# A graph network on one core: the first stage's edge network moves from the first edge pass into the pass that sorts the edges

## The chip, the cores and the metric

The kernel runs on one core of a Trainium2 chip. A core has a matrix engine (TensorE, PE), three engines for elementwise work (VectorE or DVE, ScalarE or ACT, GpSimd or POOL), an engine that mostly issues transfers (SyncE, SP) and 16 DMA engines. Each engine works through its own list of instructions in order, and waits on semaphores for the others. The metric is the device time of one execution in microseconds (us), as the median of the runs.

## The reference

There are 6,250 nodes with 48 features and 200,000 edges from `src` to `dst`. Only the first layers touch the change; shortened, they are:

```python
gate = silu(edge_attr @ F1W + F1b) @ F2W + F2b            # edge_attr: 200000 x 40, gate: 200000 x 48
gate = gate + (emb[z[src]] * (emb[z[dst]] @ adapt)).sum(-1, keepdims=True)
cw   = where(d < 6, 0.5 * (cos(pi * d / 6) + 1), 0)
agg  = segment_sum(gate * h[dst] * (cw * mult[dst])[:, None], src)
h    = layernorm(h + agg / tot)
for i in range(4):                                        # attention over the edges of each src
    score = (Q[src] * K[dst]).sum(-1) + 0.1 * (edge_attr * Q[src][:, :40]).sum(-1) + log(mult)[dst]
    h = layernorm(h + leaky(concat(h, softmax_sum(score, h[dst] @ Wm)) @ Wu))
...
x = layernorm(x + h)       # then an edge MLP and two weighted sums over the edges, by dst
```

Everything is float32. The "edge network" below is the first line: 40 numbers per edge to 48 hidden numbers, Silu, and 48 gate numbers.

## The kernel before

Edges lie on 128 partitions with J = 1,564 columns each, so one column is 128 edges. The input is in order of `dst`; the sums over `src` need the edges in order of `src`. The kernel therefore sorts the edges once, and afterwards takes every sum over a node's edges as a running scan along the sorted columns.

*The counting pass* (0 to 559 us; `sort`, `counted` L309, `early` L629). DVE compares 16 columns at a time with the node numbers (L303 `ol`, L306 `oh`) and PE counts (L316). Between these steps the generator `early` is advanced one `yield` per step: it searches where the runs of equal `dst` begin (`dst_runs`), clears the table `seed` with 17 DMAs of 3.7 MB on SP's queue, orders nodes (`dst_order`), makes one row of 81 numbers per node (`node_table` L583: features times multiplicity, the projected embedding, the multiplicity; its embedding and node types are loaded on SP's queue, L589 and L601), and lets POOL scatter these rows to the place where each node's run begins in `seed` (49 indirect DMAs, line L171, from the tile `t0`).

*The scatter pass* (559 to 3,088 us; the second half of `sort`). `ranked` works on 8 columns a step: ACT copies the running counts out of PSUM (`hs`, L384), PE looks them up (`g`, L386) and adds the step's own counts (`hs_ps`, L388), DVE turns that into each edge's place (`same` L394, `pick` L397, `at` L399, `pos` L400). For every block of CS = 16 columns `whole` builds a tile `r_s` with one row per edge. `payload` loads the 40 edge numbers on SP's queue (`a_s`, L419) and ACT copies them into the rows (L421) with src, dst and distance (L422 to L424). `expanded` loads 16 columns of `seed` and spreads each run's row over the run: ACT copies into PSUM (`run_v`, L286), DVE scans (`xf`, L269), and ACT copies the result into the rows (L676). A row has 124 floats (496 B): src, dst, distance, 40 edge numbers, 81 spread numbers. POOL then scatters the 16 columns one by one to their places in the DRAM table `rows_s` (L171). `whole` is called one block ahead of its scatters, and `r_s` has three buffers. Beside it runs `beside`: the rows of the dst order (`a_d`, `r_d`, `rows_d`), clears of the `spread` tables, and 49 scatters of node embeddings in the middle. The order on each engine is fixed at build time by a scheduler, except where `tc.keep_in_program_order` is written; each engine's queue, SP's DMA issues included, is worked through in that order.

*The first edge stage* (3,088 to 4,281 us; `gated_sums`, tile pool `e0`) reads the sorted rows in parts of C = 40 columns. PE turns the 40 edge numbers and the embedding product of two columns at a time (L954), ACT copies them out (L956), PE applies the first layer to 8 columns (L963), ACT does Silu (L965), DVE copies the two embedding products under it (L966), PE applies the second layer (L973), and DVE multiplies the gate numbers in PSUM with the edge's features (L975). Before that, DVE and ACT make the cutoff factor `u` (L915 to L923), POOL multiplies it into the features (L924), and DVE scans the sources' embeddings (`qf`, L269), multiplies and sums them (L931, L933). After it DVE scans the sums (`sf`, L986), and ACT copies them to `st` (L989), written to DRAM from ACT's queue. ACT also copies the 40 edge numbers and the product to `ra` (L909), which is written to the table `rows_a` of 41 floats a row (L934). The next part's opening (`begun`) is advanced one step per `turn`.

*Attention* (4 layers, to 13.9 ms) reads `rows_a` in parts of 40 columns on SP's queue, with one POOL gather of 128 rows per column from `tab_kv` (L166), and uses the 40 edge numbers on PE (L1125). The edge MLP and the two weighted sums follow. They are not touched.

## Time and profile before

| | |
|---|---|
| median of 3 runs | 21,866.9 us (21,861.03 to 21,871.99) |
| the profiled execution: its own time, its span | 21,773.17 us, 21,771.4 us |
| busy share of the span: PE, DVE, ACT, POOL | 27%, 37%, 22%, 64% |
| mean granted TensorE clock | 0.62 of full speed |
| counting pass, 0 to 559.4 us: busy DVE, ACT, POOL | 383.3, 26.8, 141.8 us |
| scatter pass, 559.4 to 3,088 us: busy PE, DVE, ACT, POOL | 836.7, 1,413.2, 820.2, 1,574.9 us |
| first edge stage, 3,088 to 4,281 us: busy PE, DVE, ACT, POOL | 811.2, 891.9, 584.7, 136.6 us |
| attention and its node stages, 4,281 to 13,840 us: busy POOL, DVE | 6,955.8, 3,784.3 us |
| rest, 13,840 to 21,771 us: busy POOL, DVE | 5,045.5, 1,618.3 us |

The stages follow each other in time, and each has its own limit, so a busy share of the whole span says little. In the profile L12 means line 12 of the kernel; a row such as "L421 ACT r_s" is the group of instructions that this line issued on that engine. "PEld" is the loading of weights into TensorE. "issue" as the reason of a wait means that the profile shows nothing that the engine waited for, "remote" or "an unknown queue" that the releaser is not in the record.

### The profile page before, as it was taken

The page shows a single profiled execution, that of the slowest core. Times are in us where ns is not written, and L with a number is a line of the kernel's source. Part 1 is how long each engine was busy: PE and PEld are TensorE (multiplying, and loading weights), DVE is VectorE, ACT ScalarE, POOL GpSimd, SP SyncE. Part 2 cuts the span into 40 slices and gives each one's busy share as a digit, 9 for nine tenths or more (in the row PEclk, how much of TensorE's full clock was granted, in tenths as well). Part 3 has the DMA queues.
Part 4 walks back from the last instruction along what each step waited for, and adds up shares of the span by engine and source line. Part 5 has one row for each costly group of instructions (what it writes and reads, how often), then busy time and mean ns, then how long its engine had stood idle before and what let it go on. Part 6 is the DMA issues. An engine that isn't in the chain of part 4 may idle for free.

```text
span 21771.4 us, 87599 instructions
## 1 busy us (share of the span) xinstructions
PE 5782.7 (27%) x19726; PEld 3494.4 (16%) x19726; DVE 8090.9 (37%) x16421; ACT 4790.3 (22%) x6563; POOL 13854.5 (64%) x13410
## 2 busy tenths in 40 slices
PE   2332346622223222322223222245545200000000
PEld 2332334410002000200002000133333100000000
DVE  6554557644333344334333334322222211111001
ACT  0332334411111111111111111133333200001111
POOL 2666641177775777577775777644444577777777
PEclk9999995555555555555555555566666655555555
DMA  5455544332222222222222222211111111111111
GB/s 157 165 172 134 172 169 180 151 87 88 86 83 66 86 87 88 60 89 88 86 81 70 86 85 88 57 40 43 43 46 44 33 36 34 36 36 36 36 36 36
DMA packets 873560, 1792.36 MB, mean 82 GB/s; under 512 B 365490, under 2 KB 546658, under 8 KB 868034
## 3 DMA queue, kind: packets, MB, share of 16 engines
q1 hardware_dynamic: 349038, 860.63, 12.0%
q0 software_dynamic: 427520, 547.67, 10.8%
q10 hardware_dynamic: 96468, 378.32, 4.6%
q8 instruction: 167, 2.74, 0.1%
q14 instruction: 367, 3.01, 0.0%
HBM read 1144.48 MB, written 641.17 MB: 82 GB/s over the span
## 4 chain that ended last, share of the span: by engine, by line
POOL 43%; issue 21%; DVE 10%; another core or an unknown queue 10%; PE 9%; ACT 6%; DMA 1%; ACTq 0%; SPq 0%; POOLq 0%; DVEq 0%
POOL t L166 41%; PE ps L1207 2%; PE ps L1214 2%; PE ps L1222 1%; ACT run_v L286 1%; POOL own L166 1%; DVE qf L269 1%; DVE ol L303 1%; PE g L386 1%; DVE sf L986 1%; PE ps_t L1200 1%; ACT st L1230 1%; ACT st L989 1%; DVE run_v L267 1%
## 5 line engine op out<-in xcount | busy, mean ns | idle before, releaser
L166 POOL DMA_INDIRECT t<-tab_kv,other x6256 | 6576.9, 1051 | 2112.8 <-issue 2069.6
L166 POOL DMA_INDIRECT t<-tab_x,other x4692 | 4788.3, 1021 | 2605.8 <-issue 1457.2
L1124 PE MATMUL ka<-t,ident 128*128 128x480 f32 (+2 forms) x1264 | 1213.3, 1063 | 6798.6 <-DMA t<-tab_kv,other 6015.1
L1126 DVE TENSOR_TENSOR q<-qf,ka 128x480 f32<-128x480 f32 (+2 forms) x632 | 677.9, 1074 | 4126.9 <-issue 3358.9
L171 POOL DMA_INDIRECT rows_s<-r_s,scratch x1564 | 1527.9, 977 | 967.8 <-ACT r_s L421 466.7
L1124 PEld LDWEIGHTS ka<-t,ident 128*128 128x128 f32 x1264 | 316.3, 310 | 7520.9 <-issue 4273.1
L269 DVE TENSOR_TENSOR_SCAN qf<-fac,run_v 128x480 f32<-128x480 f32 (+1 forms) x943 | 1028.8, 1092 | 654.0 <-DVE run_v L267 409.8
L841 PE MATMUL cy_ps<-ident,last_s 128*48 128x128 f32 (+1 forms) x4 | 1.6, 406 | 4523.5 <-DVE last_s L275 4523.5
L1156 ACT COPY st<-m 128x40 f32<-128x40 f32 (+3 forms) x164 | 42.8, 261 | 5233.9 <-DVE sc L1129 4099.3
L386 PE MATMUL g<-hs,olt 128*128 128x49 f32 x3128 | 759.0, 418 | 1231.1 <-ACT hs L384 860.3
L286 ACT COPY run_v<-q 128x480 f32<-128x480 f32 (+1 forms) x943 | 851.7, 916 | 503.1 <-DVE qf L269 197.8
L1125 PE MATMUL ka<-r,tenth 128*128 128x400 f32 (+2 forms) x1264 | 959.7, 863 | 0.0
L1216 DVE TENSOR_SCALAR h<-ps,b 128x512 f32<-128x512 f32 x391 | 293.6, 751 | 1725.5 <-PE ps L1207 829.7
L386 PEld LDWEIGHTS g<-hs,olt 128*128 128x128 f32 x3128 | 696.1, 327 | 1283.6 <-ACT hs L384 893.0
L1304 DVE TENSOR_TENSOR run_v<-t,w_ps 128x480 f32<-128x480 f32 (+3 forms) x164 | 142.1, 912 | 1832.6 <-DMA t<-tab_x,other 1832.6
L267 DVE SCALAR_TENSOR_TENSOR run_v<-last_s,ns,run_v 128x12 f32<-128x12 f32 x480 | 98.0, 219 | 1934.1 <-issue 1280.6
L924 POOL TENSOR_TENSOR r<-r,u 128x1920 f32<-128x1920 f32 (+3 forms) x41 | 135.5, 3305 | 1034.3 <-DVE u L923 931.1
L269 DVE TENSOR_TENSOR_SCAN sf<-dec,run_v 128x480 f32<-128x480 f32 (+5 forms) x820 | 728.1, 921 | 36.1 <-remote 14.9
L841 PEld LDWEIGHTS cy_ps<-ident,last_s 128*48 128x48 f32 (+1 forms) x4 | 0.5, 126 | 4524.3 <-ACT st L1310 2261.5
L1207 PE MATMUL ps<-at,w 112*128 112x512 f32 x782 | 539.5, 779 | 506.8 <-ACT h L1209 428.3
L1155 ACT COPY st<-sf 128x1960 f32<-128x1960 f32 (+3 forms) x164 | 620.8, 3785 | 13.3 <-DVE run_v L267 11.0
L1148 DVE TENSOR_TENSOR run_v<-t,es 128x480 f32<-128x480 f32 (+2 forms) x656 | 616.1, 961 | 9.9 <-issue 5.1
(395 smaller groups left out, 15085.7 us busy)
## 6 DMA issues: line engine op xcount, KB each, us to landing
q<-spread_s SPq DMA_DIRECT2D x190, 960.0 KB
state_a<-st ACTq DMA_DIRECT2D x152, 1000.0 KB
r<-rows_a SPq DMA_DIRECT2D x152, 820.0 KB
state_h<-st ACTq DMA_DIRECT2D x114, 960.0 KB
t<-tab_kv,other POOLq DMA_INDIRECT x6256
r<-rows_s SPq DMA_DIRECT2D x38, 2480.0 KB
t<-tab_x,other POOLq DMA_INDIRECT x4692
seed<-zeros SPq DMA_DIRECT2D x17, 3726.0 KB
```

Of the source, the lines that this page charges most:

```text
L166: return nc.gpsimd.indirect_dma_start(out=dst, out_offset=None, in_=table, in_offset=bass.IndirectOffsetOnAxis(ap=idx, axis=0))
L171: i = nc.gpsimd.indirect_dma_start(out=table, out_offset=bass.IndirectOffsetOnAxis(ap=idx, axis=0), in_=src, in_offset=None)
L269: V.tensor_tensor_scan(flat[:, f0 * wid:(f0 + n) * wid], fac[:, :n * wid], v.rearrange("p f c -> p (f c)")[:, :n * wid], 0.0, OP.mult, OP.add)
L286: return lambda v, f0, n: S.copy(v, by_feature(src[:, :, f0:f0 + n]))
L386: T.matmul(g[:, b0 + b, :], olt[:, b0 + b, :], hs[:, b, :], start=True, stop=True)
L1124: T.matmul(ka, ident, t[:, j0:j1, 0:H], start=True, stop=False)
L1125: T.matmul(ka[:, :, 0:RBF], tenth, r[:, j0:j1, 0:RBF], start=False, stop=True)
L1126: V.tensor_mul(q[:, j0:j1, :], by_column(qf)[:, j0:j1, :], ka)
L1148: V.tensor_mul(v, by_feature(t[:, :, H + 1 + f0:H + 1 + f0 + n]), es[:, None, :].to_broadcast([P, n, wid]))
L1155: S.copy(st[:, :, 0:H + 1], by_column(sf))
L1207: T.matmul(ps, w1, at, start=True, stop=True)
L1214: T.matmul(ps, w2, h1, start=True, stop=True)
```

## The change

- The edge network moves from `gated_sums` into `expanded`. A copy of the edge numbers, transposed on the host (80 rows: two neighbouring columns of 40 numbers, by column pair, by partition), is a new input. Each block of 16 columns loads its part of it on SP's queue (`at_e`, 80 partitions), and PE, ACT, PE, ACT make the 48 gate numbers and copy them into the row tile. The first layer loses the extra rows that carried the embedding product through, and the second layer keeps one row for its bias.
- A row of `rows_s` grows from 124 to 172 floats (496 to 688 B): 40 edge numbers, then src, dst and distance, 48 gate numbers, 81 spread numbers. `a_s` and `a_d` go from two buffers to one, `r_d` from three to two.
- `gated_sums` works on parts of 32 columns (50 parts), loads floats 40 to 171 of each row (528 of 688 B), and has no PE work. POOL multiplies the cutoff factor into the features as before, and in a second instruction adds the embedding product to the gate numbers. DVE multiplies the two from SBUF. The opening of the next part (`gates`) is issued as a whole before the sums of the present one.
- `rows_a` has 40 floats a row. It is now written in the first attention layer, which loads its 160 B of each row from `rows_s` and writes them on from ACT's queue.
- In the counting pass `node_table` runs directly behind `dst_order`; its loads of the embedding and the node types go through ACT's queue, and `t0` lies in another pool. The number of `yield`s between the steps changes (22 and 18 before, 6 and 20 after).

```diff
     W0 = H + G + 1
-    WS, WD = 3 + RBF + W0, 3 + EF
-    rows_a = dram.tile([EP, RA], F32, name="rows_a")
+    WS, WD = RBF + 3 + H + W0, 3 + EF
+    O = {"s": RBF, "d": 0}
+    rows_a = dram.tile([EP, RBF], F32, name="rows_a")
     seed = dram.tile([EP + NP, W0], F32, name="seed")
...
-        a = by_columns(pool, wid, attr.shape[1], f"a_{k}", CS)
+        a = by_columns(pool, wid, attr.shape[1], f"a_{k}", CS, bufs=1)
         tc.keep_in_program_order(nc.sync.dma_start(a, pj(attr)[:, s, :]))
-        r = by_columns(pool, wid, rows[k].shape[1], f"r_{k}", CS, bufs=3)
-        tc.keep_in_program_order(S.copy(r[:, :, 3:3 + attr.shape[1]], a))
-        S.copy(r[:, :, 0], ends[k][:, s])
-        S.copy(r[:, :, 1], ends["d" if k == "s" else "s"][:, s])
-        S.copy(r[:, :, 2], ew[:, s])
+        r = by_columns(pool, wid, rows[k].shape[1], f"r_{k}", CS, bufs=3 if k == "s" else 2)
+        o, f0 = (RBF, 0) if k == "s" else (0, 3)
+        tc.keep_in_program_order(S.copy(r[:, :, f0:f0 + attr.shape[1]], a))
+        S.copy(r[:, :, o], ends[k][:, s])
+        S.copy(r[:, :, o + 1], ends["d" if k == "s" else "s"][:, s])
+        S.copy(r[:, :, o + 2], ew[:, s])
...
-    def node_table(pool, psum):
+    def node_table(pool, psum, t0):
         V.tensor_mul(t0[:, :, 0:H], x, mult[:, :, None].to_broadcast([P, NB, H]))
         S.copy(t0[:, :, W0 - 1], mult)
         both = pool.tile([NEL, 2, G], F32, name="both")
-        nc.sync.dma_start(both[:, 0], A["L0_gnn_emb"])
+        nc.scalar.dma_start(both[:, 0], A["L0_gnn_emb"])
...
-            nc.sync.dma_start(z, bass.AP(tensor=types.tensor, offset=types.offset + b0 * P, ap=[[0, P], [1, 7 * P]]))
+            nc.scalar.dma_start(z, bass.AP(tensor=types.tensor, offset=types.offset + b0 * P, ap=[[0, P], [1, 7 * P]]))
...
-        for _ in range(22):
+        t0 = hp.tile([P, NB, W0], F32, name="t0")
+        yield from node_table(hp, psum, t0)
+        for _ in range(6):
             yield
         next(search)
-        yield from node_table(hp, psum)
-        for _ in range(18):
+        for _ in range(20):
...
-    def expanded(pool, psum):
+    def expanded(pool, psum, net_psum):
+        hid = [pool.tile([2 * H + 1, 4, P], F32, name=f"hid{i}", bufs=1) for i in range(2)]
+        for t in hid:
+            V.memset(t, 1.0)
         fac = factors(pool, "fac", SG, CS)
         first = pool.tile([P, 1, W0], F32, name="first", bufs=1)
         gather(first[:, 0, :], tab0[:], ends["d"][:, 0:1])
@@ -668,7 +671,18 @@
             wid = r.shape[1]
             t = by_columns(pool, wid, W0, "seeds", CS)
             tc.keep_in_program_order(nc.sync.dma_start(t, pj(seed[0:EP, :])[:, j0:j0 + wid, :]))
-            fac_, x0 = fac(j0 // CS, nsd[:, j0:j0 + wid]), 3 + RBF
+            at = pool.tile([2 * RBF, CS // 2, P], F32, name="at_e")[:, :wid // 2, :]
+            tc.keep_in_program_order(nc.sync.dma_start(at, A["edge_attr_40_t"][:, j0 // 2:(j0 + wid) // 2, :]))
+            for i, (k0, n) in enumerate(blocks(4, 0, wid // 2)):
+                ps = net_psum.tile([2 * H, 4, P], F32, name="ps_1")[:, :n]
+                T.matmul(ps, f1w, at[:, k0:k0 + n], start=True, stop=True)
+                hi = hid[i % 2][:, :n]
+                S.activation(hi[0:2 * H], ps, AF.Silu, bias=f1b)
+                ps = net_psum.tile([P, 4, 2, H], F32, name="ps_2")[:, :n]
+                for k in range(n):
+                    T.matmul(ps[:, k], hi[:, k, :], f2, start=True, stop=True)
+                S.copy(r[:, 2 * k0:2 * (k0 + n), RBF + 3:RBF + 3 + H], ps.rearrange("p k t w -> p (k t) w"))
+            fac_, x0 = fac(j0 // CS, nsd[:, j0:j0 + wid]), RBF + 3 + H
...
+    C0 = 32
     def gated_sums(ep, psum):
-        hid = [ep.tile([2 * H + 3, 4, P], F32, name=f"hid{i}", bufs=1) for i in range(2)]
-        for t in hid:
-            V.memset(t, 1.0)
         prev, f = segments_begin("s", ep)
-        factor = factors(ep, "fac")
+        factor = factors(ep, "fac", cols=C0)
         before = {"q": first_rows(ep, tab_q, "first"), "s": None, "prev": prev}
-        X0 = 3 + RBF
...
+        N0, X0 = 3, 3 + H
+        B0 = X0 + H
+        parts = [(c0, C0) for c0 in range(0, J - C0, C0)] + [(J - J % C0, J % C0 - 12), (J - 12, 12)]
+        def gates(c):
+            c0, wid = parts[c]
             s = slice(c0, c0 + wid)
-            r = by_columns(ep, wid, WS, "r")
-            nc.sync.dma_start(r, pj(rows["s"][:])[:, s, :])
-            q = by_columns(ep, wid, H, "q")
+            r = by_columns(ep, wid, WS - RBF, "r", C0, bufs=3)
+            nc.sync.dma_start(r, pj(rows["s"][:])[:, s, RBF:])
+            q = by_columns(ep, wid, H, "q", C0)
             nc.sync.dma_start(q, pj(spread["s"][0:EP, :])[:, s, :])
             before["prev"] = segments_chunk(c0, wid, r, before["prev"])
-            ra = by_columns(ep, wid, RA, "ra")
-            S.copy(ra[:, :, 0:RBF], r[:, :, 3:X0])
             fac, first = factor(c, ns[:, s]), ns[:, c0:c0 + 1]
-            kept[c] = r, ra, fac, first
-            yield
-            u = ep.tile([P, C], F32, name="u")[:, :wid]
+            u = ep.tile([P, C0], F32, name="u")[:, :wid]
             V.tensor_scalar(u, r[:, :, 2], 1.0 / (2.0 * CUT), None, op0=OP.mult)
-            n = ep.tile([P, C], F32, name="n", bufs=1)[:, :wid]
+            n = ep.tile([P, C0], F32, name="n", bufs=1)[:, :wid]
             V.tensor_scalar(n, u, ROUND, None, op0=OP.add)
             V.tensor_scalar(n, n, -ROUND, None, op0=OP.add)
             V.tensor_sub(u, u, n)
             V.tensor_mul(u, u, u)
             V.tensor_scalar(u, u, -1.0, 1.0, op0=OP.mult, op1=OP.add)
             V.scalar_tensor_tensor(u, r[:, :, 2], CUT, u, op0=OP.is_lt, op1=OP.mult)
-            nc.gpsimd.tensor_tensor(r[:, :, X0:X0 + H], r[:, :, X0:X0 + H], u[:, :, None].to_broadcast([P, wid, H]),
...
+            x_ = r[:, :, X0:B0]
+            nc.gpsimd.tensor_tensor(x_, x_, u[:, :, None].to_broadcast([P, wid, H]), op=OP.mult)
+            qf = by_features(ep, G, wid, "qf", C0, bufs=1)
+            runs(psum, qf, fac, first, before["q"], G, copied(q), cols=C0)
             before["q"] = kept_last(ep, qf, "last_q")
-            yield
...
+            V.tensor_mul(q[:, :, :G], by_column(qf), r[:, :, B0:B0 + G])
+            pair = ep.tile([P, C0], F32, name="pair")[:, :wid]
+            V.tensor_reduce(pair, q[:, :, :G], AX.X, OP.add)
+            g = r[:, :, N0:X0]
+            nc.gpsimd.tensor_tensor(g, g, pair[:, :, None].to_broadcast([P, wid, H]), op=OP.add)
+            return r, fac, first
+        def sums(c, r, fac, first):
+            c0, wid = parts[c]
+            v = by_features(ep, H + 1, wid, "v", C0)
+            S.copy(v[:, H, :], r[:, :, WS - RBF - 1])
+            V.tensor_mul(by_column(v)[:, :, 0:H], r[:, :, N0:X0], r[:, :, X0:B0])
             if before["s"] is not None:
                 V.scalar_tensor_tensor(v[:, :, 0], before["s"], first, v[:, :, 0], op0=OP.mult, op1=OP.add)
-            sf = by_features(ep, H + 1, wid, "sf", bufs=1)
+            sf = by_features(ep, H + 1, wid, "sf", C0, bufs=1)
             flat, values = (t.rearrange("p f c -> p (f c)") for t in (sf, v))
             for f0 in range(0, H + 1, FG):
                 j = slice(f0 * wid, min(f0 + FG, H + 1) * wid)
                 V.tensor_tensor_scan(flat[:, j], fac[:, :j.stop - j.start], values[:, j], 0.0, OP.mult, OP.add)
             before["s"] = kept_last(ep, sf, "last_s")
-            st = by_columns(ep, wid, H + 1, "st", bufs=1)
+            st = by_columns(ep, wid, H + 1, "st", C0)
             S.copy(st, by_column(sf))
-            nc.scalar.dma_start(pj(state0[0:EP, :])[:, s, :], st)
+            nc.scalar.dma_start(pj(state0[0:EP, :])[:, c0:c0 + wid, :], st)
+        ahead = gates(0)
+        for c in range(len(parts)):
+            now = ahead
+            if c + 1 < len(parts):
+                ahead = gates(c + 1)
+            sums(c, *now)
         return f, before["prev"], before["s"]
...
-                r = by_columns(ep, wid, RA, "r")
-                nc.sync.dma_start(r, pj(rows_a[:])[:, s, :])
+                r = by_columns(ep, wid, RBF, "r")
+                if l == 0:
+                    nc.sync.dma_start(r, pj(rows["s"][:])[:, s, 0:RBF])
+                    nc.scalar.dma_start(pj(rows_a[:])[:, s, :], r)
+                else:
+                    nc.sync.dma_start(r, pj(rows_a[:])[:, s, :])
...
-                    T.matmul(ka[:, :, 0:RBF], tenth, r[:, j0:j1, 0:RBF], start=False, stop=True)
+                    T.matmul(ka[:, :, 0:RBF], tenth, r[:, j0:j1, :], start=False, stop=True)
...
+        elif name == "edge_attr_40_t":
+            a = _np.ascontiguousarray(padded(a, EP, 0).reshape(P, J // 2, 2 * RBF).transpose(2, 1, 0))
```

## The prediction

> **What bounds the kernel now.** I read the page first: its chain of waits and its costliest groups.
>
> ```profile
> PE 5782.7 (27%) x19726; PEld 3494.4 (16%) x19726; DVE 8090.9 (37%) x16421; ACT 4790.3 (22%) x6563; POOL 13854.5 (64%) x13410
> ...
> POOL t L166 41%; PE ps L1207 2%; PE ps L1214 2%; PE ps L1222 1%; ACT run_v L286 1%; POOL own L166 1%; DVE qf L269 1%; DVE ol L303 1%; PE g L386 1%; DVE sf L986 1%; PE ps_t L1200 1%; ACT st L1230 1%; ACT st L989 1%; DVE run_v L267 1%
> ...
> L171 POOL DMA_INDIRECT rows_s<-r_s,scratch x1564 | 1527.9, 977 | 967.8 <-ACT r_s L421 466.7
> ```
>
> POOL is busy for 64% of the span, but almost all of that is gathers in the attention and edge stages after 4,281 us, which keep their form. The third line is the scatter pass (559 to 3,088 us), the stage into which the edge network moves: 1,564 scatters of 0.977 us, and before 88 of its 98 blocks POOL waits for ACT's last write of the block's row tile (L421), 466.7 us in total. Then the table of stretches (columns: stretch, length, busy us and count for PE, PEld, DVE, ACT, POOL, then TensorE clock, DMA share, GB/s):
>
> ```profile
> 559.00:1000.00 441.00, 149.22 (x822) 138.04 (x822) 250.96 (x854) 145.43 (x328) 271.73 (x278) 1.00 0.50 167
> 1000.00:1500.00 500.00, 175.46 (x968) 162.12 (x967) 296.52 (x1010) 170.28 (x381) 315.09 (x323) 1.00 0.53 173
> ...
> 1900.00:3088.00 1188.00, 405.50 (x2232) 375.09 (x2232) 683.25 (x2332) 398.48 (x896) 746.28 (x764) 1.00 0.50 163
> ...
> 3200.00:4200.00 1000.00, 691.84 (x2343) 474.14 (x2342) 751.70 (x1215) 500.05 (x608) 115.64 (x34) 0.59 0.45 181
> ```
>
> The first three rows are the scatter pass: no engine is full, PE is busy 35% of the time and its clock is 1.00. The last is the first edge stage (`gated_sums`, 3,092 to 4,281 us): DVE is busy 75% of the time, PE 69%, at clock 0.59. Its chain of waits repeats at L989 at 3,618.44, 3,648.33 and 3,678.20 us: 29.9 us for each part of 40 columns. Third, the timeline of one block of the scatter pass:
>
> ```profile
> 1006.04 0.32 PE L388 MATMUL hs_ps<-oh,ol 128*128 128x49 bf16 x4 [1.27 <-DVE oh L306]
> ...
> 1011.79 0.95 POOL L171 DMA_INDIRECT rows_s<-r_s,scratch  x1 [0.30 <-issue]
> 1015.13 0.32 ACT L384 COPY hs<-hs_ps 128x196 f32<-128x196 f32 x1 [9.76 <-remote]
> ...
> 1015.66 0.92 ACT L676 COPY r_s<-xf 128x432 f32<-128x432 f32 x1
> ...
> 1016.48 0.74 ACT L421 COPY r_s<-a_s 128x640 f32<-128x640 f32 x1
> ...
> 1017.50 0.96 POOL L171 DMA_INDIRECT rows_s<-r_s,scratch  x1 [4.75 <-ACT r_s L421]
> ```
>
> PE issues its four short `hs_ps` products at 1006.04. ACT can read them only at 1015.13, after 9.76 us of waiting, 2.4 us after the last scatter of the burst has ended (1012.74). From there it takes two copies to finish the next row tile, and the next burst starts at 1017.50. The chain shows the same wait ending at 1040.34 and 1065.12. I cannot see why PE's signal is late; I only see that it is tied to the end of the burst. So a block costs the burst (16 scatters 1.26 us apart, 20.2 us), 2.4 us until ACT is released, and what ACT still has to write: 24.8 us. ACT's idle 9.76 us are the slack in which added work can hide; work ordered behind that wait is paid in full. Last, the groups of the edge stage between 3,200 and 4,200 us:
>
> ```profile
> L973 PE MATMUL ps<-f,hid 99*128 99x96 f32 x1337 | 327.5, 426 | 114.3 <-DVE hid L966 114.3
> ...
> L963 PE MATMUL ps<-at,f1w 82*98 82x512 f32 x336 | 289.5, 960 | 1.5 <-ACT at L956 1.5
> ...
> L924 POOL TENSOR_TENSOR r<-r,u 128x1920 f32<-128x1920 f32 x34 | 117.5, 3457 | 895.1 <-DVE u L923 842.3 <-ACT run_v L286 52.8
> L966 DVE COPY hid<-ps 2x512 f32<-2x512 f32 x168 | 117.1, 697 | 175.3 <-ACT hid L965 172.1
> L965 ACT ACTIVATE hid<-ps,f1b 96x512 f32<-96x512 f32 x169 | 115.1, 681 | 31.4 <-PE ps L963 23.2 <-ACT v L945 7.9
> ...
> L931 DVE TENSOR_TENSOR q<-qf,r 128x1280 f32<-128x1280 f32 x33 | 86.6, 2624 | 0.0
> ...
> L933 DVE TENSOR_REDUCE ra<-q 128x40 f32<-128x1280 f32 x33 | 49.1, 1487 | 1.0
> L275 DVE COPY last_q<-qf 128x32 f32<-128x32 f32 x34 | 39.9, 1173 | 0.0
> ...
> L275 DVE COPY last_s<-sf 128x49 f32<-128x49 f32 x34 | 7.1, 208 | 1.2
> ```
>
> **The change part by part.** *Edge stage, the saving.* Twenty transposes, five copies, five hidden layers, five Silu, the `hid` copies (L966), twenty f2 products, five PSUM products (L975), the 1.56 us `ra` copy and the `rows_a` write all go. The part is now 32 columns and DVE is its longest engine. Per part: other and ns 0.54 (0.171+0.152+0.221); seven u operations 1.29; qf scans of 384, 384 and 256 elements, interpolated between 1.135 (480) and 0.821 (320), 2.59; three first-column updates at 0.23, 0.69; last_q 0.2; q product 0.8×2.624=2.10; reduction 0.8×1.487=1.19; the new v product from SBUF, 1,536 elements at L931's 2.05 ns, 3.15; its first column 0.32; sf scans 4×0.95+0.24=4.04; last_s 0.21. Sum 16.3 us. POOL's product grows from one to two, each 0.8×3.457=2.77 us. The trace shows what POOL can do to DVE: `last_q` takes 1.173 us against 0.208 for the larger `last_s`, because it starts while L924 runs and ends with it (3607.54). In the new order the v product and scans of the previous part stand right behind the reduction that starts POOL's second product, so I charge one full POOL product: 19.1 us. Before: 1,564/40×29.9=1,169 us. After: 1,564/32×19.1=933. Saving 236 us. Bounds: no collision, 16.3 us, saves 372; DVE only as full as now (75%), 21.7 us, saves 109.
>
> Here a rule speaks against the change. The Trainium skill (SBUF — State Buffer, "Who interferes with whom") says that a DVE instruction with two SBUF inputs contends with a GpSimd instruction that reads SBUF, and the later one fully blocks. The new v product and the sf scans are of that kind. By it both POOL products would be charged, 21.8 us a part, and the saving would be about 100 us. The trace has only the copy meeting POOL.
>
> The row load reads 132 of 172 floats, 4,096 pieces of 528 B. Row and data of the part come to 3.75 MB in 19.1 us, 196 GB/s, against 181 now; it is loaded ahead, so I charge 0. If pieces are slow, the load caps the saving (rival 3).
>
> *Scatter pass, the cost.* Per block of 16 columns: one SP load (80 partitions × 4 KB, 327 KB), two f1w products, two Silu, eight f2 products, two copies of 384 elements from PSUM. Estimated from the rows: f1w two records, 1.71 us in the chain at clock 0.59, so 1.0 at 1.00; Silu 0.68; f2 1.84 for eight records, so 1.1; copy 0.80 (run_v's 432 take 0.89). A group in series is 3.6 us, a block 7.2. The Silu and the copies wait for PE, and behind them in ACT's queue stand the `hs` and xf copies, for which PE's next products and the next burst wait; f1w waits for `at_e` with `g` and `hs_ps` behind it. Lower bound: all of it inside ACT's 9.76 idle us, 0. Upper: all in series behind the release, 98×7.2=706 us. A gain is excluded: nothing that delays PE's signal is removed. In between I use the written order of ACT, which repeats every five blocks. Behind the release, beyond today's copies, stand: one xf copy (0.93); nothing; a PSUM copy that first waits for f2 and an xf copy (3); a whole run of copies, xf, Silu and next-row numbers (about 11); nothing. Mean 3 us. I add 0.3 for the wider rows: 688 B instead of 496, while a scatter now lands 2.1 us after issue (bounds 0 and 0.8, if landing scales by 1.39). So 3.3 us × 98 = +323 us. POOL issues each scatter as before.
>
> On SP, `at_e` waits for PE and the row input `a_s` (now one buffer) for ACT's copy; behind them stand the krow and lrow loads that DVE's comparisons need. Those already wait for DVE two steps earlier, so 0; if SP stalls, the load time of 2 to 3 us a block shows, inside the same upper bound. The extra issue, 98×0.32=31 us, lies on an idle queue.
>
> *Counting pass.* `node_table` comes earlier, and its emb and types loads leave SP (where they stood behind 17 clears of 3.7 MB until 213 us) for ACT's queue. DVE sets the end of this pass: after 420 us it is busy 130.9 of 139. Its work is unchanged, so 0; bounds −40 (the two 18 to 20 us waits for PE beside the seed scatters) and +25 (types landing late beside the clears in front of DVE's comparisons). Four missing small weight loads: 0 to −3, taken as 0.
>
> *Attention, first layer.* 41 loads of 5,120 pieces of 160 B replace contiguous ones, and the `rows_a` write of the edge stage comes here, on ACT's queue, with all ACT work of a part behind it. A part takes 55.6 us (18 in 1,000 us), POOL is busy 76%, ACT 17%, DMA share 0.29. Taken +5; bounds 0 and 41×2.5=100 if the pieces delay gathers.
>
> Sum: −236+323+0+5=+92 us, 21,773+92=21,865 for an execution like the profiled one. That one lies 94 us below the median of 21,867 (three runs within 11 us); on the median's scale 21,959.
>
> **The rivals.**
> 1. *The network hides (faster).* ACT's 9.76 us are longer than 7.2. If the network runs entirely in front of the late `hs`, a block pays 0 to 1 us. Then −236+50+5: 21,690; with the uncollided edge stage 21,550. For it: DVE, the fullest engine there (59%), gets nothing new. Against: the order of ACT above. The turn is at 236/98=2.4 us a block.
> 2. *Much slower, by the TensorE clock.* At 69% PE load the clock fell from 1.00 to 0.59 within 100 us of the edge stage; at 35% it held. The network takes PE to about 52% of a block. At 0.59 PE would need (8.7+4.2)/0.59=21.9 of 25 us; three more us a block, 98×3=294, on top: 22,250. Or handshakes slip behind the late signal one after another, up to the bound of 706: 22,340. Against: 35% held for 2,500 us.
> 3. *The edge stage gains nothing much*, since loads or the POOL collision set 22 us a part: saving 100, with the scatter cost 323: 22,095.
>
> **How the numbers follow.** Scatter cost and edge saving decide. Forecast (2.5 to 5 us a block) 0.42; rival 1 0.34; rival 2 0.14; rival 3 0.10. About 0.2% (44 us) is what a measurement here tells from no change. With 236 us saved the forecast runs from +14 to +259, so I put a fifth of it, 0.08, within 44 us, and 0.34 above. Slower: 0.34+0.14+0.10=0.58; faster 0.34; same 0.08. Range: 21,590 (rival 1, a little above its best) to 22,350 (rival 2's bound); the forecast alone 21,850 to 22,250.
>
> **What would show it.** Right: bursts of `rows_s` 27 to 30 us apart instead of 24.8, POOL's wait behind L421 replaced by ACT writes of r_s from PSUM or xf, and its total rising from 467 to about 790 us; the edge stage's `st` 18 to 20 us apart with the v product stretched beside POOL. Wrong: bursts still 25 us apart (rival 1), a granted clock below 0.9 before 3,000 us (rival 2), or `st` 22 us and more apart with idle DVE waiting for r (rival 3). The whole would be wrong if PE's signal were no longer tied to the burst's end: then the pass could approach its 20.2 us bursts, and no row of this trace prices that.

## The result, and the profile after

The changed kernel takes 21,917.8 us (median of 13 runs, 21,903.2 to 21,930.3), the kernel before 21,867.3 us (13 runs, 21,856.0 to 21,896.1) beside it: ratio 1.0020, 95% interval 1.0012 to 1.0029. It is 50 us slower, where the prediction said 92. The profiled execution of the changed kernel took 21,915.7 us, close to its median; that of the kernel before lay 94 us below its own, so I took a second profile of the kernel before (run r1: 21,868.1 us, span 21,866.3) and compare with that one.

From the page of the changed kernel: busy time, the clock in 40 slices, and the group of the scatters.

```profile
PE 5653.7 (26%) x18944; PEld 3361.3 (15%) x18944; DVE 8082.2 (37%) x16312; ACT 4678.3 (21%) x6585; POOL 14029.4 (64%) x13469
...
PEclk9999999965555555555555555567666655555555
...
L170 POOL DMA_INDIRECT rows_s<-r_s,scratch x1564 | 1533.2, 980 | 1349.7 <-ACT hs L383 703.3
```

The clock stays at 1.00 until the attention begins (slice 9); with the edge network gone from it, the edge stage runs without PE. POOL's wait in front of the scatters is now put down to ACT's `hs` copy at L383, 703.3 us, where L421 stood with 466.7. The stretches (columns as before: PE, PEld, DVE, ACT, POOL, clock, DMA share, GB/s):

```profile
1000.00:1500.00 500.00, 267.97 (x1167) 211.44 (x1164) 253.84 (x867) 177.36 (x399) 268.90 (x274) 1.00 0.53 170
...
1900.00:3475.00 1575.00, 811.35 (x3520) 638.97 (x3519) 757.57 (x2586) 539.51 (x1201) 851.36 (x869) 1.00 0.53 162
...
3700.00:4375.00 675.00, 0.92 (x2) 0.36 (x2) 672.81 (x1034) 215.74 (x263) 218.95 (x76) 1.00 0.68 198
```

In the scatter pass PE is busy 54% (35% before), DVE 51% (58% in the second profile of before). In the edge stage (last row) DVE is busy all the time.

First and last scatter, for the second profile of the kernel before and for the changed kernel (count, shortest, median, longest ns, first and last start):

```profile
L171 POOL DMA_INDIRECT rows_s<-r_s,scratch x1564: 952/958/1457, 556.4 to 3135.1; - x196
```

```profile
L170 POOL DMA_INDIRECT rows_s<-r_s,scratch x1564: 954/960/1491, 562.6 to 3475.4; - x196
```

| stage, us | before (r1) | after | difference | predicted |
|---|---|---|---|---|
| counting pass, to the first scatter | 556.4 | 562.6 | +6 | 0 |
| scatter pass, first to last scatter | 2,578.7 | 2,912.8 | +334 | +323 |
| edge stage, to its last `st` copy | 1,194.6 | 900.1 | −295 | −236 |
| rest of the span | 17,536.6 | 17,538.4 | +2 | +5 |

So the parts have the signs that were predicted, the scatter pass has its size too, and what the prediction lacked is 59 us in the edge stage; the two passes took 17 of them back.

One block of the scatter pass in the changed kernel, from the timeline:

```profile
1013.03 1.99 PE L683 MATMUL ps<-f,hid 97*128 97x96 f32 x8
...
1014.81 1.92 PE L678 MATMUL ps<-at_e,f1w 80*96 80x512 f32 x2
...
1020.40 0.96 POOL L170 DMA_INDIRECT rows_s<-r_s,scratch  x1 [0.30 <-issue]
1023.55 0.49 ACT L684 COPY r_s<-ps 128x384 f32<-128x384 f32 x1 [9.94 <-remote]
...
1024.66 2.02 PE L683 MATMUL ps<-f,hid 97*128 97x96 f32 x8 [7.94 <-ACT hid L680]
...
1026.72 0.49 ACT L684 COPY r_s<-ps 128x384 f32<-128x384 f32 x1 [2.11 <-PE ps L683]
1027.10 0.32 ACT L383 COPY hs<-hs_ps 128x196 f32<-128x196 f32 x1
...
1027.62 0.94 ACT L690 COPY r_s<-xf 128x432 f32<-128x432 f32 x1
...
1028.44 0.73 ACT L421 COPY r_s<-a_s 128x640 f32<-128x640 f32 x1
...
1029.45 0.95 POOL L170 DMA_INDIRECT rows_s<-r_s,scratch  x1 [8.09 <-ACT r_s L421]
```

PE issues the first group's f2 products (L683) and the second group's f1w products (L678) by 1014.81, some 2 us long each. ACT's copy of the first gate numbers (L684) starts only at 1023.55, 2.2 us after the last scatter of the burst has ended. From there ACT needs the copy, a Silu, a second round through PE (L683, 2.02 us), another copy, `hs`, an xf copy and the attribute copy: 5.9 us from the release to the next burst, where it was 2.4 before (5.9 to 8.9 us over the blocks between 1,000 and 1,500 us that begin with such a wait). The median block is 29.2 us (25.0 in r1).

The edge stage between 3,600 and 4,300 us (line, operation, forms, count, busy us, mean ns, idle before):

```profile
L958 DVE TENSOR_TENSOR_SCAN sf<-fac,v 128x384 f32<-128x384 f32 x155 | 279.6, 1825 | 0.0
L944 POOL TENSOR_TENSOR r<-r,pair 128x1536 f32<-128x1536 f32 x39 | 121.0, 3102 | 173.4 <-DVE pair L942 173.4
...
L951 DVE TENSOR_TENSOR v<-r 128x1536 f32<-128x1536 f32 x39 | 108.6, 2785 | 0.0
L936 POOL TENSOR_TENSOR r<-r,u 128x1536 f32<-128x1536 f32 x38 | 107.5, 2828 | 293.4 <-DVE u L934 293.4
L940 DVE TENSOR_TENSOR q<-qf,r 128x1024 f32<-128x1024 f32 x39 | 73.3, 1880 | 0.0
...
L928 DVE TENSOR_SCALAR n<-u 128x32 f32<-128x32 f32 x39 | 54.0, 1384 | 0.0
...
L929 DVE TENSOR_SCALAR n<-n 128x32 f32<-128x32 f32 x39 | 6.6, 170 | 0.0
```

A scan of 384 elements takes 1.825 us on average, where I expected 0.95, and L928, a 32-element operation, 1.384 us, while its twin L929 takes 0.170. Both are means of two kinds: 56 of the 155 scans take 3.4 us on average, the others about 0.95, and 19 of the 39 L928 take 2.66 us, the others 0.17. The parts differ too, 21.5 and 14.6 us in turn, 18.25 on average. Two stretches in time order show why, first one with a held L928, then one with held scans:

```profile
3660.05 2.80 POOL L944 TENSOR_TENSOR r<-r,pair 128x1536 f32<-128x1536 f32 x1 [4.13 <-DVE pair L942]
...
3660.23 2.65 DVE L928 TENSOR_SCALAR n<-u 128x32 f32<-128x32 f32 x1
...
4001.02 4.47 DVE L958 TENSOR_TENSOR_SCAN sf<-fac,v 128x384 f32<-128x384 f32 x3
...
4001.18 3.38 POOL L944 TENSOR_TENSOR r<-r,pair 128x1536 f32<-128x1536 f32 x1 [4.75 <-DVE pair L942]
...
4014.77 3.48 POOL L936 TENSOR_TENSOR r<-r,u 128x1536 f32<-128x1536 f32 x1 [10.21 <-DVE u L934]
...
4015.56 2.73 DVE L274 COPY last_q<-qf 128x32 f32<-128x32 f32 x1
4018.21 1.88 DVE L940 TENSOR_TENSOR q<-qf,r 128x1024 f32<-128x1024 f32 x1
```

In the first, L928 starts at 3660.23 beside a POOL product and ends at 3662.88, just behind it (3662.85). In the second, POOL's product of 1,536 elements runs from 4001.18 to 4004.56; the three scans that DVE has at the same time take 4.47 us instead of 2.8. The second POOL product ends at 4018.25, and the 32-element copy `last_q`, started at 4015.56, ends at 4018.29 with it. Counted one by one between 3,600 and 4,300 us, 77 POOL products hold up 77 DVE instructions: 56 long scans, 19 times L928, once a short scan and once `last_q`. The `qf` scans of 384 elements, which read one input from PSUM, are not held: 0.95 us in the 9 of the whole stage that meet a POOL product, 0.94 in the 85 that don't.

The runs below come from several sessions, and in some of them every kernel, the one before included, took about 18.7 ms instead of 21.8 ms; so each run is held only against the kernel before of its own session, and stage against stage of such sessions. I call the 21.8 ms sessions *late* and the 18.7 ms sessions *prompt*, for a reason that the runs show. The expectations call them "the first chip" and "the second chip", which turned out wrong: one chip was prompt in one session (r5 to r8) and late in another (r15, r16).

### The profile page after: what moved, and what is told of

Its sections match the earlier page's. It is cut to its first block, busy times and chain, and to the rows that moved or that the text cites. A ratio compares the mean times of both kernels' runs of the same rounds, so it can differ in the third digit from the quotient of the medians.

```text
span 21913.9 us, 86031 instructions
## 1 busy us (share of the span) xinstructions
PE 5653.7 (26%) x18944; PEld 3361.3 (15%) x18944; DVE 8082.2 (37%) x16312; ACT 4678.3 (21%) x6585; POOL 14029.4 (64%) x13469
## 3 DMA queue, kind: packets, MB, share of 16 engines
q0 software_dynamic: 452544, 586.11, 11.4%
## 5 line engine op out<-in xcount | busy, mean ns | idle before, releaser
L170 POOL DMA_INDIRECT rows_s<-r_s,scratch x1564 | 1533.2, 980 | 1349.7 <-ACT hs L383 703.3
L268 DVE TENSOR_TENSOR_SCAN qf<-fac,run_v 128x480 f32<-128x480 f32 (+6 forms) x970 | 1030.4, 1065 | 642.8 <-DVE run_v L266 374.3
L285 ACT COPY run_v<-q 128x480 f32<-128x480 f32 (+6 forms) x970 | 855.8, 895 | 560.3 <-DVE qf L268 254.9
L683 PE MATMUL ps<-f,hid 97*128 97x96 f32 x1564 | 399.2, 434 | 858.9 <-ACT hid L680 806.7
```

What stands on the lines that cost most here:

```text
L170: i = nc.gpsimd.indirect_dma_start(out=table, out_offset=bass.IndirectOffsetOnAxis(ap=idx, axis=0), in_=src, in_offset=None)
L268: V.tensor_tensor_scan(flat[:, f0 * wid:(f0 + n) * wid], fac[:, :n * wid], v.rearrange("p f c -> p (f c)")[:, :n * wid], 0.0, OP.mult, OP.add)
L285: return lambda v, f0, n: S.copy(v, by_feature(src[:, :, f0:f0 + n]))
L683: T.matmul(ps[:, k], hi[:, k, :], f2, start=True, stop=True)
```

## The experiments

**r1: the kernel before once more**, without an edit.

> The kernel before once more, unchanged, for a second profile. The profiled execution of the prediction lay 94 us below the median of its kernel. If that execution was an odd one, this profile has a span near 21,865 us and shows in which stages the 94 us lie; if profiles of this kernel always read 0.4% short, the span is again near 21,775 us. Its ratio to the kernel before is 1.000.

21,871.0 us, ratio 1.000 (0.999 to 1.0009); the span is 21,866.3. The profile on which the prediction rests was a short execution: of the 95 us between the two, 51 lie in the scatter pass (2,527.7 and 2,578.7 us), 3 in the edge stage, 44 in small pieces behind it, and the counting pass is 3 shorter. Putting the 94 us on top of the sum as a constant was right for the kernel's time.

**r2, r3: blocks of 8 columns**, in the kernel before and in the changed one.

```diff
-CS = 16
+CS = 8
```

> Kernel before with blocks of 8 columns instead of 16 in the scatter pass (195 bursts of 10.1 us instead of 98 of 20.2 us). Theory 1, PE's signal is held only once a burst has lasted some 12 us: no hs copy waits longer than about 2 us in a burst, the pass takes 195 x (10.1 + 1 to 2) = 2,160 to 2,360 us instead of 2,529, the kernel 170 to 370 us less. Rival, the signal is held until the end of any burst: 195 x (10.1 + 4.6) = 2,870 us, the kernel about 340 us more.

> Changed kernel with blocks of 8 columns. Theory 1 (held only in bursts over 12 us): the handovers of the edge network meet no held signal, the pass takes 195 x (10.1 + 1 to 3) = 2,160 to 2,550 us instead of 2,913, the kernel 21,370 to 21,750. Rival (held until the end of any burst): 195 x (10.1 + 5 to 9) = 2,940 to 3,700 us, the kernel 21,950 or more.

r2: 22,195.4 us, ratio 1.0149 (1.0132 to 1.0166). r3: 21,830.5 us, ratio 0.9982 (0.9972 to 0.9991).

```profile
L171 POOL DMA_INDIRECT rows_s<-r_s,scratch x1564: 952/958/1255, 561.3 to 3469.9; - x196
```

```profile
L170 POOL DMA_INDIRECT rows_s<-r_s,scratch x1564: 954/961/1440, 557.2 to 3390.0; - x196
```

For the kernel before, the rival is right: the pass takes 2,909 us, 330 more. Short bursts don't set PE's signals free. But the two kernels differ: the changed one, with more work, is 76 us shorter in the same pass (2,833), and 80 us shorter than with blocks of 16. Neither of my two theories says that. What POOL waits for between 1,000 and 1,500 us, in r2 and then in r3 (us, times, longest):

```profile
POOL rows_s L171 <- ACT hs L384: 159.1, 17, 9.4
```

```profile
POOL rows_s L170 <- ACT hs L383: 111.4, 21, 7.9
...
POOL rows_s L170 <- ACT r_s L684: 32.1, 7, 4.6
```

Two bursts of the kernel before follow each other at once and then POOL waits 9.4 us, while the changed one waits about 5 us in front of most bursts. So the two written orders give different numbers of pauses; that this is what makes the passes differ is argued, not shown.

**r4: the edge network without PE.** ACT's two Silu and two copies a block stay, on constant tiles; the gate numbers are constants.

```diff
-                T.matmul(ps, f1w, at[:, k0:k0 + n], start=True, stop=True)
+                ps = const1[:, :n]
...
-                for k in range(n):
-                    T.matmul(ps[:, k], hi[:, k, :], f2, start=True, stop=True)
+                ps = const2[:, :n]
```

> Changed kernel; the edge network's products on PE are left out of the scatter pass, ACT's two Silu and two copies a block stay and read constant tiles in PSUM (the gate numbers are constants). The load of the transposed edge numbers stays. Theory: the network costs by its handovers with PE that fall behind the late signal, so a block falls from 29.2 to 25 to 26 us and the pass by 310 to 410 us, the kernel to about 21,550. Rival: ACT's added time or the wider rows cost it, a block stays at 28 to 29 us and the kernel within 100 us of 21,918.

21,810.7 us, ratio 0.9976 (0.9966 to 0.9985).

```profile
L170 POOL DMA_INDIRECT rows_s<-r_s,scratch x1564: 954/960/1661, 557.8 to 3396.1; - x196
```

The pass takes 2,838 us, 75 less than with PE's products. By whole kernels, each against the kernel before of its own session, it is 114 us less (64 faster than before instead of 50 slower; the profiled execution of r4 lies 19 us above its median). So my theory, that the cost is PE's answers falling behind the late signal, covers 75 to 114 of 334 us. The median block is 25.9 us, as the theory said, but the blocks are no longer alike: four in a row take 20.2, 45.1, 26.8 and 20.6 us. I read this so: where a row tile is finished before the burst ends, the next burst follows at once, no pause lets PE's signals through, and the next but one waits the longer. The trace supports it only in part. Of the time that ACT spends in the scatter pass in waits over 2 us that end without a releaser, 784 of 1,226 us end in a pause of POOL (over 1 us) in r1, 872 of 975 in the changed kernel and 710 of 1,203 in r4. The others end while a burst runs, as this one in r1:

```profile
1200.83 0.96 POOL L171 DMA_INDIRECT rows_s<-r_s,scratch  x1 [0.31 <-issue]
...
1201.75 0.32 ACT L384 COPY hs<-hs_ps 128x196 f32<-128x196 f32 x1 [11.36 <-remote]
...
1202.09 0.96 POOL L171 DMA_INDIRECT rows_s<-r_s,scratch  x1 [0.30 <-issue]
```

**r5 to r8, r9 to r12, r13 to r16.** I meant these to split the rest, but the sessions of r5 to r14 were prompt, and only that of r15 and r16 was late, like that of r1 to r4. They are told by kernel.

*The changed kernel itself in a prompt session (r9).*

> The changed kernel once more, unchanged. On the first chip (before: 21,870 us) PE's signals come late while POOL scatters, on the second (before: 18,731 us) they did not. If this run falls on the second chip: the scatter pass pays only what doesn't fit beside POOL's bursts, 2,220 us as in the kernel without the pair product against 2,096 (+124), the edge stage saves 294, the kernel is about 170 us faster than before (18,560). On the first chip: 21,918 again, scatter pass 2,913, edge stage 900.

18,574.3 us against 18,720.2: ratio 0.9921 (0.9905 to 0.9938). Here the change makes the kernel 146 us faster. For the stages of before in a prompt session I use r6, which was as fast as the kernel before (first r6, then r9):

```profile
L171 POOL DMA_INDIRECT rows_s<-r_s,scratch x1564: 953/959/1647, 421.6 to 2517.9; - x196
```

```profile
L170 POOL DMA_INDIRECT rows_s<-r_s,scratch x1564: 954/960/1702, 444.6 to 2648.2; - x196
```

The scatter pass is 2,096.3 us before and 2,203.6 after, +107 instead of +334; the edge stage is 899.3 us, the same as in late sessions (1,193.5 in r6); the counting pass ends at 444.6 instead of 421.6, +23. Together −164, and the whole −146: the profiled execution of r6 lies 23 us above the median of the kernel before in r9's session. In the counting pass DVE waits 29 us for the gathers of the search in r9, 4.8 us in r6. I put that to the fewer `yield`s between the steps; no run changes them alone:

```profile
DVE got L566 <- DMA got<-steps,at: 19.0, 1, 19.0
DVE got L566 <- DMA got<-dst_steps,at: 10.3, 1, 10.3
```

*One buffer (r6).* The kernel before with `a_s` and `a_d` single and `r_d` double.

```diff
-        a = by_columns(pool, wid, attr.shape[1], f"a_{k}", CS)
+        a = by_columns(pool, wid, attr.shape[1], f"a_{k}", CS, bufs=1)
...
-        r = by_columns(pool, wid, rows[k].shape[1], f"r_{k}", CS, bufs=3)
+        r = by_columns(pool, wid, rows[k].shape[1], f"r_{k}", CS, bufs=3 if k == "s" else 2)
```

> Kernel before, with the one buffer of the changed kernel for the edge numbers (a_s, a_d) and two for r_d; nothing else. If the single buffer costs the time (SP waits for ACT's copy with the krow and lrow loads behind it), the pass grows by 100 us or more, to 2,680 us and more, and the kernel to 21,970 or more. If it doesn't, the kernel stays within 30 us of 21,867.

18,735.4 us, ratio 1.0002 (0.9992 to 1.0012), prompt. The buffers cost nothing there; in a late session it was not tried.

*No edge network at all (r5, r10, r13, r15).* The rows stay 688 B wide, DVE fills the 48 gate numbers with a constant; nothing of the network is computed.

```diff
-            at = pool.tile([2 * RBF, CS // 2, P], F32, name="at_e")[:, :wid // 2, :]
...
-                S.copy(r[:, 2 * k0:2 * (k0 + n), RBF + 3:RBF + 3 + H], ps.rearrange("p k t w -> p (k t) w"))
+            V.memset(r[:, :, RBF + 3:RBF + 3 + H], 0.5)
```

> Changed kernel with the whole edge network left out of the scatter pass (no load of the transposed numbers, no PE, no Silu, no copies; the 48 gate numbers are filled with a constant by DVE). Rows stay 688 B wide, the attribute tile stays single. Theory, ACT's four added operations a block (2.4 us of work on the in-order queue that also carries the hs copies) are the cost: a block falls back to 25 to 25.5 us, the pass to about 2,600 us, the kernel to 21,580 to 21,620. Rival, the wider rows or the single buffer cost it: the pass stays above 2,750 us and the kernel above 21,740.

> Changed kernel without the edge network in the scatter pass, the 48 gate numbers a constant. On the second chip its pass was as long as that of the kernel before (2,094 against 2,096 us): the wider rows were free there. On the first chip, if the network (and not the rows) makes the pass longer: 2,580 to 2,650 us against 2,913, the kernel at 21,580 to 21,650. If the wider rows do: above 2,800 and 21,800. On the second chip again: 18,462.

> Changed kernel without the edge network in the scatter pass, meant for the first chip (before: 21,870 us). If the network makes the pass longer there: 2,580 to 2,650 us against 2,913, the kernel at 21,580 to 21,650. If the wider rows do: above 2,800 and 21,800. On a chip like the second: 18,455 and a pass of 2,090.

> As the run of this kernel before it. On the first chip: 2,580 to 2,650 us of scatter pass and a kernel of 21,580 to 21,650 if the network makes the pass longer there, above 2,800 and 21,800 if the wider rows do. On another chip: about 18,460 and 2,090, and the point stays open.

Prompt: 18,461.9 us (ratio 0.9856, 0.9840 to 0.9873), 18,454.8 (0.9859, 0.9842 to 0.9875) and 18,475.8 (0.9857, 0.9842 to 0.9873), with passes of 2,094, 2,086 and 2,094 us. The wide rows cost nothing there; all 107 us of the prompt pass are the network. Late (r15): 21,688.7 us against 21,757.6, ratio 0.9969 (0.9953 to 0.9984). First r10, then r15:

```profile
L170 POOL DMA_INDIRECT rows_s<-r_s,scratch x1564: 956/960/1573, 441.0 to 2527.1; - x196
```

```profile
L170 POOL DMA_INDIRECT rows_s<-r_s,scratch x1564: 954/960/1642, 556.3 to 3306.5; - x196
```

In the late session the pass without the network still takes 2,750 us, between my two expectations: 163 less than the changed kernel and 171 more than the kernel before, both as profiled in other sessions. Its blocks repeat as 35.4, 25.0, 30.8, 26.4 and 20.7 us. Held against its own session the split is another. By whole kernels the network is worth 119 us (50 slower than before with it, 69 faster without), hardly more than PE's products alone in r4 (114). And the kernel before was 116 us faster in that session than in that of r1, while the span behind the edge stage was only 54 to 63 us shorter (17,473 us in r15 and 17,482 in r16, 17,537 in r1). With the other stages as measured its pass would be about 2,530 us (an estimate: 21,756 less 556, 1,195 and 17,478), so that some 220 us stay without the network.

As the same rows are free in prompt sessions, and as the scatters themselves have the same median of 960 ns, I put these 220 us to the new order on ACT, in which some tiles are finished early. This is argued, not shown: the wider rows, the single buffer and DVE's filling of the gate numbers are in r15 too, and none of them was tried alone in a late session.

*Blocks of 8 columns, two blocks ahead (r8, r12, r14, r16).* The changed kernel with CS = 8, five row tiles and:

```diff
-                ahead = whole(0)
+                ahead = [whole(0), whole(CS)]
...
-                        r = ahead
+                        r = ahead.pop(0)
...
-                    if j % CS == 0 and j + CS < J:
-                        ahead = whole(j + CS)
+                    if j % CS == 0 and j + 2 * CS < J:
+                        ahead.append(whole(j + 2 * CS))
```

> Changed kernel with blocks of 8 columns that are made two blocks ahead of their scatters instead of one, with five row tiles instead of three and two attribute tiles. If POOL's wait is only a lack of finished row tiles, the pass falls from 2,833 us (8 columns, one ahead) to 2,300 to 2,600 us, the kernel to 21,300 to 21,600. If what limits it is the time in which PE's signals come through at all, tiles in store only move the pauses: the pass stays within 60 us of 2,833 and the kernel within 60 us of 21,830.

> Changed kernel with blocks of 8 columns, made two blocks ahead. On the second chip its pass took 2,165 us, 55 less than with blocks of 16 made one ahead. On the first chip, if a store of finished tiles bridges the late signals: 2,300 to 2,600 us and 21,300 to 21,600. If the late signals only move the pauses: within 60 us of 2,833 (blocks of 8, one ahead), the kernel within 60 us of 21,830.

> Changed kernel with blocks of 8 columns, made two blocks ahead, meant for the first chip. If a store of finished tiles bridges the late signals: a pass of 2,300 to 2,600 us and 21,300 to 21,600. If the late signals only move the pauses: within 60 us of 2,833, the kernel within 60 us of 21,830. On a chip like the second: 18,530.

> As the run of this kernel before it. On the first chip: a pass of 2,300 to 2,600 us if finished tiles bridge the late signals, within 60 us of 2,833 if not. On another chip: about 18,535, and the point stays open.

Prompt: 18,537.5 us (ratio 0.9897, 0.9880 to 0.9913), 18,528.3 (0.9898, 0.9881 to 0.9914) and 18,545.4 (0.9893, 0.9877 to 0.9910); the pass is 2,155 us in r12. Late: 21,759.2 against 21,757.6, ratio 0.9999 (0.9987 to 1.0010).

```profile
L170 POOL DMA_INDIRECT rows_s<-r_s,scratch x1564: 954/960/1461, 559.9 to 3371.1; - x196
```

The late pass is 2,811 us, 22 from r3: finished tiles in store don't bridge the late signals. Each against its own session, it gains nothing over r3 with its one block ahead (level with the kernel before here, 0.2% faster there). In the prompt session this kernel is 46 us faster than the changed kernel of the same session; in late sessions it is level with the kernel before, where the changed kernel is 0.2% behind. It beats the changed kernel in both kinds, and the kernel before in one.

*No second POOL product (r7, r11).* The embedding product is not added to the gate numbers.

```diff
-            nc.gpsimd.tensor_tensor(g, g, pair[:, :, None].to_broadcast([P, wid, H]), op=OP.add)
```

> Changed kernel without POOL's second product in the first edge stage (the embedding product is not added to the gate numbers). If that product blocks DVE's scans, the sf scans fall from 1.83 to about 1.0 us, a part from 18.05 to about 15 us, the stage by 49 x 3.1 = 150 us and the kernel to about 21,770. Rival, the scans are slow for another reason (their two inputs lie in SBUF): scans and stage stay within 20 us.

> Changed kernel without POOL's second product in the edge stage. On the second chip the stage took 768 us. Theory, that product blocks DVE's scans with two SBUF inputs and nothing else in the stage depends on the chip: 768 us on the first chip as well, 132 less than the changed kernel's 900, the kernel at 21,785; on the second chip again 18,465, and the changed kernel of the same call about 130 us above it.

18,465.3 us (ratio 0.9858, 0.9841 to 0.9874) and 18,445.2 (0.9853, 0.9837 to 0.9870), prompt; r11 is 129 us below the changed kernel of its session, the stage 767.9 us instead of 899.3. The scans, in r11, and the POOL product that is left:

```profile
L957 DVE TENSOR_TENSOR_SCAN sf<-fac,v 128x384 f32<-128x384 f32 x131 | 185.1, 1427 | 0.4
L936 POOL TENSOR_TENSOR r<-r,u 128x1536 f32<-128x1536 f32 x33 | 98.4, 2982 | 405.2 <-DVE u L934 275.8 <-ACT run_v L285 80.1 <-DVE run_v L266 40.6
```

The scans fall from 1.825 to 1.427 us, not to 1.0, because 29 of them are now held by the other POOL product, of which 33 run in this stretch. A part takes 15.3 us instead of 18.2.

## Why the prediction was right or wrong

The direction was right and the sum too large: +92 predicted, +50 measured, with the measured value inside the range. (The range given for the forecast alone, 21,850 to 22,250, is wider than its own +14 to +259, which end at 21,881 and 22,126.) Point by point:

- **Counting pass, 0.** +6 in a late session. In prompt sessions it is +23: the bounds were −40 and +25, and the cause that I had in mind for the loss, types landing late (5.8 us of waits in r9), is smaller than the waits for the search's gathers (29 us). I did not look at the distance between the two halves of the search.
- **Scatter pass, +323.** +334. The step "the written order of ACT behind the release" gave 3 us a block, and what it describes is in the trace: after the release stand another round through PE and an xf copy, and the stretch from the release to the next burst grows from 2.4 to 5.9 us. But r4 and r15 show that the reasoning was luckier than the number looks. By whole kernels, each against its own session, taking away PE's products frees 114 us, taking away the whole network 119, and some 220 (an estimate) stay with an order that differs from before and has nothing to hide. So the added handovers, which the sum was made of, account for about a third, and what the rest is due to stays open. If my reading of r4 is right, counting the instructions behind the release of one block misses that a tile finished early removes the pause in which the next one is made.
- **Wider rows, 0.3 us a block inside that sum.** Nothing in prompt sessions; not tried alone in a late one.
- **Edge stage, −236.** This is the step that failed: "Sum 16.3 us", and one POOL product of 2.8 on top, 19.1 us a part. Measured 18.2, and neither half is right. Two kinds of DVE instruction are stretched by POOL: scans, by (1.825−0.95)×155/39=3.5 us a part, and L928, by 1.2; that is 4.7 us, not 2.8. The v product, which the prediction expected to be stretched beside POOL, met none (0 of 39). What remains is 13.5 us, not 16.3; r11, with one POOL product, leaves the same (15.3 less 4×0.48). The mean durations that I added overlap: four scans of 1.138 us take 4.32 us in the chain of waits of the kernel before, and the small operations start 0.1 us apart though each lasts 0.2. Then v, at 2.79 us, and q, at 1.88, cost 1.8 ns an element, not the 2.05 that I took from L931. The stage has the columns of 48.9 full parts, so 0.85 us a part (19.1−18.25) is 42 of the 59 us; the other 17 lie in the first and last parts, above all of the kernel before, whose stage took 1,194.6 us and not the 1,169 of the sum.
- **The rule of the Trainium skill** (SBUF — State Buffer, "Who interferes with whom") was right about the machine where I charged half: both POOL products hold up DVE, one instruction each time (77 and 77), and it is scans with two SBUF inputs, a copy and scalar operations. By it the collision would be 5.5 us; 4.7 was measured. Combined with the true 13.5 it would have given 19.0, with my 16.3 it gave 21.8.
- **Loads of 528 B pieces, 0.** Right: DVE is busy 100% of the time.
- **Attention, +5.** The rest of the span, attention included, moved by 2 us.
- **Rivals.** The clock (rival 2) did not fall: 1.00 through the pass with PE at 54%. Rival 1, the network that hides, is what happens in prompt sessions: +107 us, 1.1 a block, and the kernel is 146 us faster. Its turn at 2.4 us a block would be 3.0 with the 295 us that the edge stage saved; the late session's 3.4 lie above it. What it turns on is whether PE's signals are late, which I took as given.

## What to carry to other kernels

Add up start-to-start times from the chain or the timeline, not mean durations, when a stage has many short instructions on one engine; and charge a DVE stage for every POOL product that runs beside it, where the trace shows that such products hold DVE up. Where an unexplained wait carries the forecast, give both cases, with it and without it, their own sum: here it turned −0.8% into +0.2%. A cost that hangs on a pause is not found by counting what stands in the pause alone: with the network gone, the pass was still longer than before, by the estimate above, by more than the network itself was worth.

## What the runs showed of the hardware that was not expected

The same kernel has two speeds, 21.8 ms and 18.7 ms, that hold through a session, and one chip showed both. They differ in how soon PE's finished work is seen while POOL issues indirect DMAs. ACT's waits for the `hs_ps` products between 1,000 and 1,500 us, in r1 (late) and r6 (prompt), in us, times, longest:

```profile
ACT hs L384 <- remote: 235.0, 36, 11.4
...
ACT hs L384 <- PE hs_ps L388: 11.3, 8, 2.9
```

```profile
ACT hs L384 <- PE hs_ps L388: 86.3, 42, 4.0
```

In the late session 235 of 500 us are waits for a PE signal with no releaser in the record at that time, of up to 11.4 us; in the prompt one none are listed, and the longest wait for these products is 4.0 us. It is not special to the scatters: in the edge MLP, beside gathers, ACT's copy of PE's transposes (L1202) waits in r1 and r6 as follows, over 391 copies:

```profile
  remote: 496.1, 64
  PE ps_t L1200: 473.4, 275
```

```profile
  PE ps_t L1200: 447.1, 371
```

PE's first layer there (L1207) in its turn waits 1,019.3 us for ACT in r1 and 0.7 us in r6. Over the whole execution, waits of more than 0.5 us without a releaser add up to 2,941 us over all engines in r1, most of them for PE, and r6 has none. Where POOL issues no indirect DMA, the two kinds agree: the edge stage of the kernel before, with PE busy 68% of the time, takes 1,194.6 us in r1 and 1,193.5 in r6, and r1 has no such wait over 2 us in it.

What makes a session late stays open; it was not the kernel, and one chip showed both. Whether the some 220 us that r15 keeps are due to order alone stays open too.
